# Order of the first loads and operations, of one bias transpose and of the last scatters in a graph-attention and mixture-of-experts kernel

## The chip, the cores and the metric

The kernel runs on one core of a Trainium2 chip. The metric is the time of one execution on the device, in microseconds, lower is better. The core has five engines that run side by side, each in the order of its own instruction list: PE (TensorE, matrix multiplication), DVE (VectorE), ACT (ScalarE), POOL (GpSimd) and SP (SyncE, which here only issues transfers). Engines wait for one another through semaphores. Transfers (DMA) are issued from the lists of SP, ACT and POOL, and they run beside all engines.

## The reference

There are N = 4096 rows of D = 256 numbers, an adjacency matrix of N x N integers, 4 attention heads of 64 columns, and 8 experts of 1024 hidden columns, of which each row uses 2.

```
xn   = layernorm(x)
h    = xn @ W                      per head
w_ij = exp(leaky_relu(s_row_i + s_col_j)) where adj_ij > 0, else 0
out  = (w @ h) / sum_j w_ij
y    = elu(out) + xn @ Wr + br
x    = x + layernorm(y) * gamma + beta
xf   = layernorm(x)
top two experts of xf @ Wg + bg, softmax over the two
x    = x + sum over the two of  share * (gelu(xf @ W1 + b1) @ W2 + b2)
```

## The kernel before, in words

**Attention.** The rows whose attention is computed are taken in four groups of 1024 (index `a`), each of two halves of 512. For a group the kernel walks over 32 tiles `j` of 128 neighbours. For each tile SP loads a slice of the transposed adjacency matrix (`load_adj`, 512 KB), ACT makes a mask of zeros and ones from it in two passes (`load_mask`, L1092 and L1093), DVE makes the weights `w` of four heads (`weigh`, L1205), and PE adds up `acc` (L745) and the denominators `den` (L754). The weights need `er`, the row scores of the group spread over all partitions. These are stored in memory as `parts` and loaded back over all partitions (`load_rows`, L710).

The projections `h`, the scores and the residual are computed in blocks of 512 rows (index `b`). Their work is woven into the first group: block b + 2 is normalised and turned (`norm_block`: moments by BNStats at L174, an inverse root in twelve short dependent DVE steps at L157 to L166 and L562, `xn`, PE transposes `pt` at L584, copies `xT` on ACT), and block b + 1 is projected (`project_block`: `ph`, `pr`, `ha`, `rb`).

**Start.** Blocks 0 and 1 have code of their own. DVE takes the moments of block 0 while its rows arrive; PE runs 37 matmuls without use (`WARM`) meanwhile. `scores_weights` folds the score vectors into the weights and computes `limit`, a bound on the scores, by one PE product (`plim`, L513), a root, and `flag`. `project_first` projects block 0 (L658), makes the scores, stores them (`store_parts`, L703), and scales `ha` (L676). `measured(1)` takes the moments and root of block 1, and `norm_block(1)` turns it. `residual_first` makes block 0's residual `rb` (PE `pr` at L688, DVE at L692). Then the program branches on `flag` (L1129) into general code, or into the code that runs here. In it, the first group's tiles j = 0 to 3 run for the first half of the rows alone, with masks kept in part of `er1`. After block 1 is projected and its scores are stored, the second `er` load brings the other half.

**Experts.** Each row goes into the lists of its two experts in memory. Tiles of 256 or 384 listed rows (jobs) run through both products (`up` with `ph` at L1355 and gelu at L1359; `down` with `po` at L1384), DVE scales the result and adds the bias (`o`, L1393), and POOL adds it to the output rows by an indirect transfer (scatter, L1396), 128 rows each, each after the one before has landed. The fixed number of jobs (`todo`) is followed by a branch for further jobs, which isn't taken here. The last scatter of the last fixed job stands behind this branch: `down` yields before it, and the generator is taken up again at the end of the program.

**What sets the order.** A scheduler at build time puts each engine's instructions in one fixed list, by the order in which the program issues them and by what they depend on. `tc.issue_after(x)` lets a group of operations count as issued after instruction `x` in that sorting; it adds no wait. On the first 40 us each engine's list is thus the result of the order of calls in the source and of these marks. PE's order in the attention is fixed by `queue`.

Of the kernel before, what the change touches and what calls it, by code (L numbers as in the profile page):

```python
# [1 line left out]

# [7 lines left out]
F32 = mybir.dt.float32  # L10
I32 = mybir.dt.int32
BF16 = mybir.dt.bfloat16
# [29 lines left out]
def gat_then_moe(  # L42
# [92 lines left out]
    def rows_of(mat, b):  # L135
        return mat[ts(b, B), :].rearrange("(t p) d -> p t d", p=P)
# [73 lines left out]
    def loaded(name):  # L210
        return fin.tile([P, TB, D], F32, tag="loaded", name=name, bufs=2)
# [253 lines left out]
    with ExitStack() as layer:  # L465
# [60 lines left out]
        first_masks = er1[:, 0].rearrange("p h r -> p (h r)").bitcast(BF16)  # L526
        first_masks = first_masks.rearrange("p (t r) -> p t r", t=TB)

        ha = gat.tile([P, NT, HK], F32)


# [14 lines left out]

        turned = {}

        def measured(b):

            xb = loaded("xb")
            if b == 0:
                for t in range(TB):
                    nc.sync.dma_start(xb[:, t, :], x[ts(t, P), :])
            else:
                nc.sync.dma_start(xb, rows_of(x, b))
            mv = moments(xb)
            r, _ = root_of(mv[:, :, 1], TB)
            off = None
            if b < 2:  # L560
                off = sums_of("off")
                marks["off"] = nc.vector.scalar_tensor_tensor(  # L562
                    off, mv[:, :, 0], -1.0, r, op0=OP.mult, op1=OP.mult
                ).ins
            return xb, mv, r, off

        def norm_block(b, found=None):

            xb, mv, r, off = found or measured(b)
            pt = [bank([P, B], f"pt{c}") for c in range(DC)]  # L570
            for t in range(TB):
                xn = fin.tile([P, D], F32, tag="xn", name="xn", bufs=2)
                if off is not None:
                    nc.scalar.activation(
                        xn, xb[:, t, :], AF.Identity, bias=off[:, t : t + 1],
                        scale=r[:, t : t + 1],
                    )
                else:
                    nc.vector.tensor_scalar(
                        xn, xb[:, t, :], mv[:, t, 0:1], r[:, t : t + 1],  # L580
                        op0=OP.subtract, op1=OP.mult,
                    )
                for c in range(DC):
                    nc.tensor.transpose(pt[c][:, ts(t, P)], xn[:, ts(c, P)], ident)  # L584
            xT = (first_large if b < 2 else large)("xT")
            xT = xT.rearrange("p t d -> p (t d)").rearrange("p (c i) -> p c i", c=DC)
            for c in range(DC):
                marks[f"turned{b}"] = nc.scalar.activation(  # L588
                    xT[:, c, :], pt[c], AF.Copy, accum_out=sums[:, c, b : b + 1]
                ).ins  # L590
            turned[b] = xT
# [59 lines left out]
        def project_first():  # L651

            sc = small.tile([P, TB, 2 * H], F32, tag="sc", name="sc")
            cols, rows = sc[:, :, :H], sc[:, :, H:]
            phs = [acc[t // 2][t % 2][:, : HK + 2 * H] for t in range(TB)]
            for t in range(TB):
                for c in range(DC):
                    nc.tensor.matmul(  # L658
                        phs[t], turned[0][:, c, ts(t, P)], wall[:, c, :],
                        start=(c == 0), stop=(c == DC - 1),  # L660
                    )
                nc.vector.tensor_tensor(rows[:, t], phs[t][:, HK + H :], limit, OP.add)
                nc.vector.tensor_tensor(
                    cols[:, t], phs[t][:, HK : HK + H], limit, OP.subtract
                )
            part = small.tile([P, H, TB], F32, tag="part", name="part")
            nc.vector.tensor_scalar(
                part.rearrange("p h t -> p t h"), rows, 0.0, None, op0=OP.max
            )
            nc.scalar.activation(part, part, AF.Exp, scale=SLOPE - 1.0)  # L670
            store_parts(0, part, nc.sync)
            ed = unit[:, :TB, :, 1]
            nc.scalar.activation(ed, cols, AF.Exp, scale=SLOPE)
            nc.scalar.activation(eb[:, :TB, :], cols, AF.Exp, scale=1.0 - SLOPE)
            for t in range(TB):
                marks["h"] = nc.vector.tensor_tensor(  # L676
                    ha[:, t, :].rearrange("p (h k) -> p h k", h=H),
                    phs[t][:, :HK].rearrange("p (h k) -> p h k", h=H),
                    ed[:, t].unsqueeze(2).to_broadcast([P, H, K]), OP.mult,
                ).ins  # L680
# [403 lines left out]
            last[0] = None  # L1084
            listed.clear()

        def load_mask(a, j, am=None):

            at = load_adj(gat, range(a * R, (a + 1) * R), j, 1, 3)
            if am is None:  # L1090
                am = gat.tile([P, R], BF16, tag="am", name="am", bufs=3)
            nc.scalar.activation(am, at[:, 0], AF.Relu)  # L1092
            nc.scalar.activation(am, am, AF.Sign)  # L1093
            return am


        idle = bank([P, B], "idle")
        for i in range(WARM):
            nc.tensor.matmul(
                idle, all1, all1[:, :1].to_broadcast([P, B]), start=(i == 0), stop=(i == WARM - 1)  # L1100
            )


        warm = gat.tile([P, 1], F32)
        nc.scalar.activation(warm, tiny, AF.Exp)
        marks = {}
        norm_block(0)
        with tc.issue_after(marks["off"]):
            scores_weights()
        project_first()  # L1110
        with tc.issue_after(marks["turned0"]):
            for j in range(2):
                load_mask(0, j, first_masks[:, j])
        with tc.issue_after(marks["flag"]):
            second = measured(1)

            nc.vector.tensor_scalar(brm, brm, -1.0, None, op0=OP.add)
            made_of_numbers()
        with tc.issue_after(marks["h"]):
            norm_block(1, second)  # L1120
            residual_first()
        load_rows(er0[:, :1], 0, 1, nc.sync)
        rest_of_loads()
        general = nc.values_load(
            flag[0:1, 0:1], min_val=0, max_val=1,
            skip_runtime_bounds_check_because="a comparison gives 0 or 1",
# [65 lines left out]
        with chosen.Else():  # L1192
# [4 lines left out]
            with tc.tile_pool(name="sep", bufs=2) as work:  # L1197
# [13 lines left out]
                    return w  # L1211

                both = list(range(HB))
                turn_biases()
                ers = [er0, er1]
                er = er0
                pending = None
                for a in range(NR):
                    later = None
                    for j in range(NT):  # L1220
                        if a == 0 and j % TB == 0 and j // TB + 2 < NB:
                            norm_block(j // TB + 2)
                        if a == 0 and j < TB:

                            am = first_masks[:, j]
                            if j > 1:
                                load_mask(a, j, am)
                            attend(weigh(er, am, j, [0]), j, [0])
                            if j == TB - 1:
                                project_block(1, True)  # L1230
                                load_rows(er[:, 1:], 1, 1, nc.sync)
                                for i in range(TB):
                                    attend(weigh(er, first_masks[:, i], i, [1]), i, [1])
                            continue
                        if a == 0 and j % TB == 0 and j // TB + 1 < NB:
                            project_block(j // TB + 1, True)
                        attend(weigh(er, load_mask(a, j), j, both), j, both)
                        if pending and j:
                            next(pending, None)
                            if j % 2 and a + 1 == NR:  # L1240
                                next(pending, None)
                        if a + 1 == NR and j == 29:
                            first_tile()
                        if j == 20 and a + 1 < NR:
                            later = ers[(a + 1) % 2]
                            load_rows(later, (a + 1) * HB, HB, nc.scalar)
# [116 lines left out]

    rounds, optional = [0], [False]

    def down(job, hT):


# [8 lines left out]
        for k in range(nch):  # L1377
# [8 lines left out]
                ))  # L1386
            if k + 1 == nch:
                yield
            if job["last"] and k + 1 == nch:
                o = work.tile([CH, D], F32, name="o_last", bufs=1)  # L1390
            else:
                o = work.tile([CH, D], F32, tag="o", name="o", bufs=2 * LAG - 2)
            given_out.append(nc.vector.scalar_tensor_tensor(  # L1393
                o, po, share[:, k : k + 1], b2s[k], op0=OP.mult, op1=OP.add
            ).ins)
            nc.gpsimd.indirect_dma_start(  # L1396
                job["into"], bass.IndirectOffsetOnAxis(ap=ids[:, k : k + 1], axis=0), o, None,
                compute_op=OP.add,
            )

    fresh()
    ordered[0] = True
# [102 lines left out]
```

## Time and profile before

| | us |
|---|---|
| time, median of 3 runs | 1325.94 |
| lowest, highest | 1325.19, 1327.08 |
| span of the profiled execution | 1330.1 |
| first scores weighted (`w`, L1205) | 34.81 |
| end of the attention, start of the experts | about 826 |
| last scatter starts | 1324.69 |

The profile is one execution, and its span is the frame of all times below. "Busy" is the share of the span in which an engine executes. In the slices each digit is a fortieth of the span (33 us), in tenths. In a chain of work each line is a start, a duration and what ran or was waited for; "issue" is time in which an engine waited for nothing that the profile shows. In a timeline a line is a start, a duration, the engine, the line of the program, what is written from what, and in brackets how long the engine had been idle and who ended that.

### The profile page before, as it was taken

The numbers are of one execution on the slowest core, as the hardware profiler recorded it, in microseconds if no ns is written. First come the engines' busy times: TensorE is split into PE (matmuls) and PEld (weight loads), VectorE is DVE, ScalarE is ACT, GpSimd is POOL, SyncE is SP. The second block draws the span as 40 slices with busy tenths as digits, with TensorE's granted clock in tenths as the row PEclk, the third lists the DMA queues.
The fourth block names the chain that finished last, engine by engine and source line by source line (L and its number), as shares of the span: only waits on it lengthen the run. The fifth ranks groups of instructions, "written<-read, shape, count | busy, mean of one in ns | idle before, by whom it ended". The sixth has DMA issues, their size and how long they took to land.

```text
span 1330.1 us, 19232 instructions
## 1 busy us (share of the span) xinstructions
PE 1287.9 (97%) x7019; PEld 679.3 (51%) x7019; DVE 868.8 (65%) x1746; ACT 574.1 (43%) x1016; POOL 232.5 (17%) x190
## 2 busy tenths in 40 slices
PE   6899999999999999999999999999999999999997
PEld 4423344322232222232222323888888877888886
DVE  4899887789999989999899996655111111121110
ACT  3423333346764457644576432533333332323332
POOL 1000000000005300015000150125222222122222
PEclk9899999999999999999999999999899999999999
DMA  5525243343443535534333342987756786888772
GB/s 164 204 84 174 96 111 96 112 158 100 131 136 109 194 98 140 138 107 153 96 111 111 106 133 60 350 249 213 245 155 188 189 183 146 197 203 209 175 208 53
DMA packets 144145, 202.42 MB, mean 152 GB/s; under 512 B 49728, under 2 KB 113872, under 8 KB 143392
## 3 DMA queue, kind: packets, MB, share of 16 engines
q1 hardware_dynamic: 122448, 161.26, 40.7%
q0 software_dynamic: 19360, 32.53, 10.9%
q10 hardware_dynamic: 2224, 7.22, 1.4%
q8 instruction: 59, 0.97, 0.3%
q14 instruction: 54, 0.44, 0.1%
HBM read 171.89 MB, written 29.08 MB: 151 GB/s over the span
## 4 chain that ended last, share of the span: by engine, by line
PE 57%; DMA 19%; DVE 17%; issue 5%; ACT 1%; another core or an unknown queue 0%; POOLq 0%; ACTq 0%; DVEq 0%
PE acc L745 24%; DMA out<-o,ids 18%; PE den L754 12%; DVE w L1205 12%; PE po L1384 8%; PE ph L1355 7%; PE pr L629 1%; PE ph L605 1%; DMA xb<-in_x 1%; DVE y L983 1%; DVE y L975 1%; PE pt L584 1%; DVE y L972 1%; PE pt L1337 1%; DVE y L989 0%
## 5 line engine op out<-in xcount | busy, mean ns | idle before, releaser
L1205 DVE SCALAR_TENSOR_TENSOR w<-er,eb,am 128x1024 f32<-128x1024 f32 x496 | 610.0, 1286 | 44.5 <-PE den L754 41.3
L745 PE MATMUL acc<-w,ha 128*64 128x512 f32 x2048 | 466.2, 599 | 5.3 <-DVE w L1205 4.6
L745 PEld LDWEIGHTS acc<-w,ha 128*64 128x64 f32 x2048 | 137.7, 137 | 301.6 <-issue 281.0
L1359 ACT ACTIVATE hT<-ph,bias 128x256 f32<-128x256 f32 (+1 forms) x264 | 126.3, 480 | 296.5 <-PE ph L1355 205.2
L1092 ACT ACTIVATE am<-adj 128x1024 bf16<-128x1024 int32 x124 | 131.1, 1057 | 283.8 <-DVE w L1205 275.2
L1355 PE MATMUL ph<-xT,w 128*128 128x256 f32 (+1 forms) x1056 | 242.3, 387 | 4.0 <-ACT hT L1359 2.5
L754 PE MATMUL den<-w,unit 128*2 128x512 f32 x2048 | 238.2, 592 | 5.5 <-DVE w L1205 5.5
L1384 PE MATMUL po<-w,hT 128*128 128x256 f32 x1088 | 241.9, 381 | 0.0
L1384 PEld LDWEIGHTS po<-w,hT 128*128 128x128 f32 x1088 | 206.7, 191 | 28.2
L1355 PEld LDWEIGHTS ph<-xT,w 128*128 128x128 f32 x1056 | 200.5, 190 | 39.4 <-ACT hT L1359 3.1
L1393 DVE SCALAR_TENSOR_TENSOR o<-po,share,b2s 128x256 f32<-128x256 f32 x67 | 32.3, 483 | 268.3 <-PE po L1384 246.8
L1396 POOL DMA_INDIRECT out<-o,ids x67 | 104.9, 1566 | 345.0 <-DMA out<-o,ids 215.6
L754 PEld LDWEIGHTS den<-w,unit 128*2 128x2 f32 x2048 | 43.5, 84 | 174.5 <-issue 151.8
L1093 ACT ACTIVATE am<-am 128x1024 bf16<-128x1024 bf16 x124 | 130.9, 1057 | 3.0
L909 POOL DMA_INDIRECT lists<-xe,at x64 | 92.0, 1437 | 134.3 <-DVE missed L888 39.5
L993 POOL DMA_DIRECT2D out<-y x6 | 4.7, 782 | 329.3 <-issue 155.6
L1341 DVE COPY xT<-pt 128x256 f32<-128x256 f32 x13 | 5.5, 423 | 66.3 <-PE pt L1337 66.3
L605 PE MATMUL ph<-wall,xT 128*128 128x264 f32 x112 | 30.6, 393 | 0.3 <-DVE sc L615 0.3
L1376 ACT ACTIVATE b2s<-b2b,share 128x256 f32<-128x256 f32 x68 | 30.8, 503 | 0.0
L629 PE MATMUL pr<-wr,xT 128*128 128x256 f32 x112 | 29.0, 384 | 0.2 <-ACT xT L588 0.2
L187 ACT ACTIVATE m<-y,off 128x256 f32<-128x256 f32 x48 | 23.8, 497 | 10.5 <-DVE off L184 10.5
L962 ACT ACTIVATE y<-ptr,z 128x64 f32<-128x64 f32 x96 | 22.0, 313 | 8.7 <-PE ptr L960 8.7
(316 smaller groups left out, 655.8 us busy)
## 6 DMA issues: line engine op xcount, KB each, us to landing
w<-in_L_ffn_W SPq DMA_DIRECT2D x66, 1024.0 KB
adj<-in_adj SPq DMA_DIRECT2D x128, 512.0 KB
er<-parts ACTq DMA_DIRECT2D x3, 2048.0 KB
b2b<-in_L_ffn_b SPq DMA_DIRECT2D x33, 128.0 KB
early<-lists SPq DMA_DIRECT2D x16, 260.0 KB
residual<-rb POOLq DMA_DIRECT2D x8, 512.0 KB
rb<-residual SPq DMA_DIRECT2D x8, 512.0 KB
out<-y POOLq DMA_DIRECT2D x8, 512.0 KB
```

Of the source, the lines that this page charges most:

```text
L605: nc.tensor.matmul(ph, xT[:, c, ts(t, P)], wall[:, c, :], start=(c == 0), stop=(c == DC - 1),)
L629: nc.tensor.matmul(pr[:, t % 2, :], xT[:, c, ts(t, P)], wr[:, c, :], start=(c == 0), stop=(c == DC - 1),)
L745: queue(nc.tensor.matmul(acc[half][h // 2][ts(h % 2, K), :], ha[:, j, ts(h, K)], w[half][h], start=(j == 0), stop=(j == NT - 1),))
L754: queue(nc.tensor.matmul(den[h * Q : h * Q + HB, :], unit[:, j, h, 1 - half : 1 - half + HB], w[half][h], start=(j == 0 and half == 0), st ...
L909: ins = nc.gpsimd.indirect_dma_start(lists, bass.IndirectOffsetOnAxis(ap=at[:, k, t : t + 1], axis=0), xe[:, t, :], None,).ins
L1092: nc.scalar.activation(am, at[:, 0], AF.Relu)
L1093: nc.scalar.activation(am, am, AF.Sign)
L1205: nc.vector.scalar_tensor_tensor(wh[:, these], er[:, these, h], eb[:, j, h : h + 1], mask[:, these], op0=OP.max, op1=OP.mult,)
L1355: order_of(nc.tensor.matmul(ph, job["w1"][:, c, ts(f, P)], xT[:, c, :], start=(c == 0), stop=(c == DC - 1),))
L1359: job["gelu"] = nc.scalar.activation(hT[:, f, :], ph, AF.Gelu, bias=job["bias"][:, f : f + 1]).ins
L1384: order_of(nc.tensor.matmul(po, hT[:, f, ts(k, CH)], w2[:, f, :], start=(f == 0), stop=(f == FC - 1)))
L1396: nc.gpsimd.indirect_dma_start(job["into"], bass.IndirectOffsetOnAxis(ap=ids[:, k : k + 1], axis=0), o, None, compute_op=OP.add,)
```

## The change

1. On SP, block 1's rows are loaded (`rows_loaded(1)`) ahead of the adjacency tiles j = 0 and 1. The tiles j = 2 and 3 of the first group, loaded after the branch before, are loaded at the start in one transfer of 1 MB, into a free half of `er1` (`first_adj`). `load_mask` is split so that the masks can be made from either place.
2. The matmuls without use become `warm_up`, which writes to `acc[1][1]` instead of a bank of its own; four more stand behind row tile 1's transposes of block 0 and two more behind row tile 3's. In PE's list `plim` is now behind all transposes of block 0.
3. `ha` of block 0 goes into `factor_first`, behind block 1's moments and root in DVE's list.
4. `residual_first` is called before `norm_block(1)`: in PE's list its eight `pr` products stand ahead of block 1's transposes.
5. `rest_of_loads` gets a mark; its place in POOL's list stays the same.
6. `turn_biases` (one PE transpose and one DVE copy) moves from just behind the branch into the second group, a = 1, at j = 1.
7. The last job's first scatter is held back until the branch for further jobs is passed, and goes out just ahead of the last one. It gets an output tile of its own, and the other `o` tiles have 9 buffers instead of 10.

```diff
+        first_adj = er1[:, 1].rearrange("p h r -> p (h r)").bitcast(I32)
+        first_adj = first_adj.rearrange("p (t r) -> p t r", t=2)
...
+        def warm_up(n):
+            idle = acc[1][1]
+            for i in range(n):
+                nc.tensor.matmul(
+                    idle, all1, all1[:, :1].to_broadcast([P, B]), start=(i == 0), stop=(i == n - 1)
+                )
...
+                if b == 0 and t % 2:
+                    with tc.issue_after(ins):
+                        warm_up(5 - t)
...
         norm_block(0)
+        second = rows_loaded(1)
         with tc.issue_after(marks["off"]):
             scores_weights()
         project_first()
+        with tc.issue_after(marks["off"]):
+            ats = [load_adj(gat, range(R), j, 1, 3) for j in range(2)]
+            nc.sync.dma_start(first_adj, adjT[2 * P : 4 * P, :R].rearrange("(t p) i -> p t i", p=P))
         with tc.issue_after(marks["turned0"]):
             for j in range(2):
-                load_mask(0, j, first_masks[:, j])
+                mask_of(ats[j][:, 0], first_masks[:, j])
         with tc.issue_after(marks["flag"]):
-            second = measured(1)
+            second = measured(1, second)
             nc.vector.tensor_scalar(brm, brm, -1.0, None, op0=OP.add)
             made_of_numbers()
+        with tc.issue_after(marks["off"]):
+            factor_first()
         with tc.issue_after(marks["h"]):
+            residual_first()
             norm_block(1, second)
-            residual_first()
         load_rows(er0[:, :1], 0, 1, nc.sync)
-        rest_of_loads()
+        with tc.issue_after(marks["turned0"]):
+            rest_of_loads()
...
-                turn_biases()
...
                             if j > 1:
-                                load_mask(a, j, am)
+                                mask_of(first_adj[:, j - 2], am)
...
+                        if a == 1 and j == 1:
+                            turn_biases()
...
             if k + 1 == nch:
                 yield
-            if job["last"] and k + 1 == nch:
-                o = work.tile([CH, D], F32, name="o_last", bufs=1)
+                while job["last"] and held_back:
+                    held_back.pop(0)()
+            if job["last"]:
+                o = work.tile([CH, D], F32, name=f"o_last{k}", bufs=1)
             else:
-                o = work.tile([CH, D], F32, tag="o", name="o", bufs=2 * LAG - 2)
+                o = work.tile([CH, D], F32, tag="o", name="o", bufs=2 * LAG - 3)
...
-            nc.gpsimd.indirect_dma_start(
-                job["into"], bass.IndirectOffsetOnAxis(ap=ids[:, k : k + 1], axis=0), o, None,
+            add = partial(
+                nc.gpsimd.indirect_dma_start, job["into"],
+                bass.IndirectOffsetOnAxis(ap=ids[:, k : k + 1], axis=0), o, None,
                 compute_op=OP.add,
             )
+            if job["last"] and k + 1 < nch:
+                held_back.append(add)
+            else:
+                add()
```

## The prediction

> **What bounds the kernel now.** I read the page first (busy shares, then the slices), next the chain of work in order of time for the first 40 us and for the end, and then the timeline of single engines there. The sums below are made against the profiled span, 1330.1 us; the three timed runs have a median of 1325.94 us (1325.19 to 1327.08), so I carry differences over and not totals. A timed change of 0.2%, 2.7 us, is about what these runs can tell from none.
>
> ```profile
> span 1330.1 us, 19232 instructions
> PE 1287.9 (97%) x7019; PEld 679.3 (51%) x7019; DVE 868.8 (65%) x1746; ACT 574.1 (43%) x1016; POOL 232.5 (17%) x190
> PE   6899999999999999999999999999999999999997
> DVE  4899887789999989999899996655111111121110
> ```
>
> PE is nearly always busy except in the first slice and the last; DVE is as full as PE through the attention (to about 826 us). Work that both start earlier therefore ends earlier: the place to look is the beginning. The chain there, then DVE's timeline:
>
> ```profile
> 23.49 0.69 PE pt L584 x2
> 24.17 0.85 PE pr L688 x2
> ...
> 28.21 2.01 PE pr L688 x8
> 30.22 0.02 issue
> 30.25 0.56 DVE rb L692
> 30.80 0.08 issue
> 30.88 0.07 DVEq L1129
> 30.95 3.75 issue
> ...
> 34.81 0.75 DVE w L1205
> ```
>
> ```profile
> 20.73 0.18 DVE L667 TENSOR_SCALAR part<-sc 128x16 f32<-128x16 f32 x1
> ...
> 22.64 0.16 DVE L562 SCALAR_TENSOR_TENSOR off<-mv,r 128x4 f32<-128x4 f32 x1
> 28.02 0.69 DVE L692 TENSOR_TENSOR rb<-pr,brm 128x512 f32<-128x512 f32 x1 [5.22 <-PE pr L688]
> 30.25 0.69 DVE L692 TENSOR_TENSOR rb<-pr,brm 128x512 f32<-128x512 f32 x1 [1.53 <-PE pr L688]
> 34.81 0.75 DVE L1205 SCALAR_TENSOR_TENSOR w<-er,eb,er 128x512 f32<-128x512 f32 x1 [3.87 <-issue]
> ```
>
> To be seen: DVE's last work before the branch (L1129) is the residual of block 0, `rb`. It waits 5.22 + 1.53 us for PE, whose `pr` matmuls stand between and behind block 1's transposes `pt`, and those wait for block 1's root (`off`, 22.64). Only after the branch and 3.75 us without an instruction can the first `w` start. The DMA rate falls to 8 GB/s between 27 and 28 us, so the 1 MB load of `er` (issued 23.21) has landed by then and is not what DVE waits for.
>
> The end, first the chain, then POOL's timeline:
>
> ```profile
> 1286.42 36.37 DMA out<-o,ids
> 1322.79 0.10 POOLq L1465
> ```
>
> ```profile
> 1308.53 1.54 POOL L1396 DMA_INDIRECT out<-o,ids  x1 [2.86 <-DMA out<-o,ids]
> 1317.93 1.55 POOL L1396 DMA_INDIRECT out<-o,ids  x1 [7.87 <-DVE o L1393]
> 1324.69 1.54 POOL L1396 DMA_INDIRECT out<-o_last,ids  x1 [5.21 <-issue]
> ```
>
> The scatter issued at 1317.93 lands at 1322.79; only then does POOL leave the branch, and the last scatter starts 1.90 us later, though its data `o_last` was written from 1320.79 on. From there to the end it is 1330.1 - 1324.69 = 5.4 us.
>
> **What the Trainium skill says.** "Runtime: NRT & Kernel Launch", section Instruction fetch mechanics: a taken branch to code outside the pages held forces a fetch before execution goes on. The trace agrees: 3.75 us on DVE here, and SP's branch at 24.1 is followed by its next load at 28.73. It gives no price, so I use 3.75. "TensorE: Matmul & The Clock Gate", What's actually happening: an idle PE drops to half clock and needs a busy window to return; the trace shows a granted clock of 0.54 from 36 to 41 us and 1.00 from 41 to 50. "DMA: Bandwidth & Descriptors", Rules for kernel authors: an accumulating DMA must wait for an earlier one on the same bytes; the trace agrees (42 scatters waited for the one before), so the last two stay serial.
>
> **The change, part by part.** Orders are those of the two built programs.
>
> *Loads.* On SP, block 1's `x` (512 KB) moves ahead of the two adjacency loads, and a 1 MB load for j = 2, 3 follows them. Before, it was issued at 6.86 and kept DVE waiting 1.72 us (to 16.92). The new order issues it at about 5.1, so it no longer binds. The extra 1 MB takes about 3 us at the 343 to 377 GB/s seen there and is in by about 18, under the projection and ahead of the `er` load. POOL's five small loads keep their place: 0.
>
> *Warm-ups.* Six more, at 10.75/37 = 0.29 us each. Four stand before the transposes of rows 2 and 3, which waited till 13.49 for their input and for `plim` anyway: 0 to +0.1. Two stand before `plim`, now last: it runs at about 14.75 and not 13.05, so DVE's root and `flag` end near 17.0 instead of 15.20, and BNStats of block 1 starts at 17.0 (before 16.92, for the DMA). The earlier load's gain is thus spent: 0.
>
> *Roots ahead of h.* From 17.0 DVE runs four BNStats (0.40 each), the score pairs (0.14) and `brm` (0.26) interleaved; PE's eight projections (3.96 us, from 15.1) end at 19.05. The last pair is at 19.4 and `part` at 19.6 (before 20.73: -1.1). Twelve dependent root steps at 0.20 end `off` at 21.9 (before 22.80: -0.9). Then four `ha` (1.42) to 23.4.
>
> *Residual ahead of block 1's transposes.* PE does `pp` at 20.0 and eight `pr`: 16 records at 0.22 to 0.25 = 3.5 to 4.0 us, from 20.3 to about 24.1. DVE's `rb` run 23.4 to 24.0 and 24.15 to 24.8. DVE branches at about 24.9 instead of 30.88: **-6.0**. Block 1's transposes follow on PE and ACT only; their second bank waits for the first `rb` (24.0), and ACT ends near 27.9 (before 28.74). SP stores `parts` 1.25 us earlier (20.6) and `er` lands at about 25.8, before it is needed; POOL's store of `rb` (512 KB, 31.24) moves ahead with its data to about 25.2 and has nothing behind it until block 1's. With the same 3.75 us of fetch the first `w` starts at 29.0 instead of 34.81: **-5.8**. The biases' copy leaves DVE here (0.14) and returns in the second attention block behind `z`, where DVE is the bound, with one 0.24 us matmul and a 0.22 us copy: net +0.1 to +0.4, taken as +0.2.
>
> *From there to the second half of the rows.* ACT's four mask passes (1.05 each) after its branch end near 36; the first is needed by the ninth `w`, at 36.1: just in time. SP's two `x` and six adjacency loads leave from 27.5 at 300 to 400 GB/s; none is needed before about 33. DVE's order up to the stored scores of block 1 holds 16 half `w` (0.65), two blocks' moments, eight normalisations and two roots, as before, but some eight root steps fewer ahead of it: before, 34.81 to 59.31 = 24.5 us; now about 23.5. `part` of block 1 comes at about 52.6 (before 59.31: -6.7). SP then issues block 5's `x`, when block 3's rows are normalised, and the second `er` load:
>
> ```profile
> 61.78 0.39 SPq L556 DMA_DIRECT2D xb<-in_x  x1
> 62.22 0.82 SPq L710 DMA_DIRECT2D er<-parts  x1
> ```
>
> These move to about 54.7 and 55.3. `x` lands 4.7 us later as before (66.44), and 2.7 us of DVE work lead to `w` on the new rows, which started at 69.04: now about 62. From this `w` on both programs issue the same instructions on DVE and PE, except for the biases, so the shift of **-7.0** stays to the end. PE's own limit caps the gain: in the stretches from 40 to 80 it was idle 1.34 + 0.77 + 1.36 = 3.5 us, so 5.8 + 3.5 = 9.3 is the most.
>
> *Tail.* The first of the last job's scatters moves behind the branch. POOL then leaves the branch when the scatter of 1308.53 has landed (about 4.9 us later, 1313.4) plus 1.9, at 1315.3, ahead of the data (1317.65). The first scatter starts at 1317.93 as before and lands at 1322.79; the next waits for that alone, and such pairs follow at 0.75 us (landing to start elsewhere in the chain): 1323.54 instead of 1324.69, **-1.1**. One `o` buffer fewer (9): comparing each `o` with the landing nine scatters earlier leaves at least 33 us; 0.
>
> Sum: -7.0 + 0.2 - 1.1 = -7.9, 1322.2 of the profiled span, or 1325.94 - 7.9 = **1318 us**.
>
> **The rivals.**
> A, the sum above: 0.65, own range 1316 to 1320.
> B, half the start comes back: `ha` and `rb` go out earlier, but masks j = 2, 3 or the fetch are late. The fetch was 4.6 us on SP under load against 3.75; ACT's masks have no slack. Each us late costs one; at 3 to 4 us, 1321.5. 0.18.
> C, the start was hidden: then only the tail counts, 1325 (same). For it: DVE and PE both fill the first block. Against: both start earlier. 0.09.
> D, slower: PE's clock. After the branch PE is fed by DVE and starts cold again after some 4 us of idling. If it stays at half clock, some 30 us of PE work up to 62 us become the bound. Each us at half clock loses 0.5 us; the gain of 7.9 and PE's 2 us of slack are gone after about 20 us more at half clock, and 30 us more make 1331. Against: before, the clock was back within 5 us. 0.05.
> That the held scatter delays the end is smaller: the first would have to start after 1319.1 to lose anything, and after 1327 to undo the start, against 1315.3 for POOL's exit. With other losses it makes 0.03, on the slower side too.
>
> **How the numbers follow.** A and B are faster: 0.83, and C's better half adds 0.03: 0.86. C's rest is the same, 0.06; D and the tail are slower, 0.08. Range: 1314.5 (PE's limit, 9.3 + 1.1, and the timed spread) to 1322.5 (B's worse end); outside it lie C, D and little else.
>
> **What would show it.** Right: DVE's `rb` of block 0 ahead of 25 us, first `w` at about 29, `w` on the second rows at about 62, later groups of equal duration; the last two scatters 5.6 us apart, the second starting 6 us before the end. Wrong: `rb` still waiting for PE after 27, BNStats of block 1 after 18, ACT's masks or PE's granted clock holding `w` between 30 and 60, or POOL's first held scatter more than 1 us after its `o`.

## The result

The changed kernel takes 1320.08 us (median of 4 runs, 1317.26 to 1321.65) against 1325.57 us for the kernel before (median of 4, 1324.7 to 1327.08). The ratio is 0.9955, with a 95% interval of 0.9935 to 0.9975. A second measurement beside three experiments gave 0.9941 (0.9922 to 0.9960). So it is faster by about half a per cent; 1318 was forecast.

The page of the changed kernel, its span, busy shares and the slices of PE and DVE:

```profile
span 1319.9 us, 19242 instructions
PE 1284.2 (97%) x7025; PEld 677.7 (51%) x7025; DVE 868.7 (66%) x1746; ACT 574.4 (44%) x1016; POOL 232.8 (18%) x190
PE   7999999999999999999999999999999999999996
DVE  6899877789999989999899997665111111121110
```

PE is as full as before in every slice but the first and the last. The two profiled spans are 10.2 us apart, more than the medians, and not all of that is the change's. About 5 to 6 us are one stall in the profiled execution of the kernel before, among the experts, here in its chain of work:

```profile
928.14 0.47 ACT hT L1359
928.61 3.12 another core or an unknown queue
931.73 0.03 issue
931.76 0.48 ACT hT L1359
```

ACT stood 3.12 us for something the trace does not name, and PE, idle meanwhile, came back at a lower clock (0.65 to 0.67 from 930 to 940 us). From the first `pt` of the experts to the end of PE's last `po` that execution needs 493.8 us; all others profiled for this study, experiment 8 apart, need 487.7 to 489.0. Later times of the kernel before are therefore compared as differences from a point of the same execution.

**The start.** DVE's timeline and the chain of work of the changed kernel:

```profile
18.88 0.18 DVE L688 TENSOR_SCALAR part<-sc 128x16 f32<-128x16 f32 x1
...
21.13 0.16 DVE L579 SCALAR_TENSOR_TENSOR off<-mv,r 128x4 f32<-128x4 f32 x1
...
22.54 0.68 DVE L717 TENSOR_TENSOR rb<-pr,brm 128x512 f32<-128x512 f32 x1
24.08 0.69 DVE L717 TENSOR_TENSOR rb<-pr,brm 128x512 f32<-128x512 f32 x1 [0.87 <-PE pr L713]
```

```profile
24.72 0.07 DVEq L1160
24.79 3.29 issue
28.08 0.05 DVEq L1236
28.13 0.06 issue
28.19 3.41 DVE w L1236 x5
31.60 0.09 issue
31.69 3.68 PE acc L770 x8
35.38 2.97 PE den L779 x16
```

DVE branches at 24.72 (30.88 before) and starts `w` at 28.19 (34.81 before), 6.6 us earlier. But the chain then hands over to PE, whose first `acc` starts at 31.69, only 4.7 us earlier than before (36.41), although it needs no more than the second `w`, which ended at about 29.5. (Before, it had started 0.1 us behind the second `w`.) PE's timelines, one line of the kernel before and two of the changed one, put the wait down to `w`:

```profile
36.41 3.68 PE L745 MATMUL acc<-w,ha 128*64 128x512 f32 x8 [3.10 <-DVE w L1205]
...
25.12 0.93 PE L601 MATMUL pt<-ident,xn 128*128 128x128 f32 x4 [0.64 <-ACT xn L591]
31.69 3.68 PE L770 MATMUL acc<-w,ha 128*64 128x512 f32 x8 [5.64 <-DVE w L1236]
```

What really held it is in the records of the branch on the engines' sequencers (duration as minimum, median and maximum in ns, then the start in us); the first line is of the kernel before, the rest of the changed one:

```profile
L1129 PEldq COMPARE_BRANCH  x1: 3931/3931/3931, 28.9 to 28.9; - x1
...
L1160 SPq COMPARE_BRANCH  x1: 45/45/45, 23.2 to 23.2; - x1
L1160 DVEq COMPARE_BRANCH  x1: 72/72/72, 24.7 to 24.7; - x1
L1160 POOLq COMPARE_BRANCH  x1: 50/50/50, 25.6 to 25.6; - x1
L1160 PEldq COMPARE_BRANCH  x1: 5317/5317/5317, 26.2 to 26.2; - x1
```

PE's branch begins at 26.2 and takes 5.32 us (28.9 and 3.93 before): PE is ready for its next instruction at 31.5. Just ahead of it POOL had issued the store of block 0's residual, 512 KB (POOL's timeline):

```profile
25.07 0.79 POOL L720 DMA_DIRECT2D residual<-rb  x1 [19.16 <-DVE rb L717]
```

**The end.** POOL's timeline:

```profile
1303.04 1.54 POOL L1440 DMA_INDIRECT out<-o,ids  x1 [2.98 <-DMA out<-o,ids]
1309.23 1.55 POOL L1424 DMA_INDIRECT out<-o_last,ids  x1 [4.65 <-issue]
1314.42 1.54 POOL L1440 DMA_INDIRECT out<-o_last,ids  x1 [3.64 <-issue]
```

The last two scatters are 5.19 us apart instead of 6.76. But the one before them starts 7.05 us after the start of its `o` (1295.99), where it was 1.71 us before the change, so POOL leaves the branch late and the first held scatter starts 2.4 us after its data are complete (1306.37 + 0.48). From the end of PE's last `po` (1309.71) it is 10.2 us to the end of the span, against 9.6 before.

### The profile page after: what moved, and what is told of

The parts are those of the page before. It is cut to its first block, busy times and chain, and to the rows that moved or that the text cites. A ratio compares the mean times of both kernels' runs of the same rounds, so it can differ in the third digit from the quotient of the medians.

```text
span 1319.9 us, 19242 instructions
## 1 busy us (share of the span) xinstructions
PE 1284.2 (97%) x7025; PEld 677.7 (51%) x7025; DVE 868.7 (66%) x1746; ACT 574.4 (44%) x1016; POOL 232.8 (18%) x190
## 4 chain that ended last, share of the span: by engine, by line
PE 60%; DMA 17%; DVE 16%; issue 4%; ACT 1%; POOLq 0%; ACTq 0%; DVEq 0%; SPq 0%
PE acc L770 24%; DMA out<-o,ids 15%; PE den L779 12%; DVE w L1236 12%; PE ph L1387 9%; PE po L1418 9%; PE pr L650 1%; PE ph L626 1%; DMA adj<-in_adj 1%; DVE y L1008 1%; DVE y L1000 1%; DMA er<-parts 1%; DVE y L997 1%; PE pt L1369 1%; DVE y L1014 0%
## 5 line engine op out<-in xcount | busy, mean ns | idle before, releaser
L1410 ACT ACTIVATE b2s<-b2b,share 128x256 f32<-128x256 f32 x68 | 30.8, 503 | 0.0
L626 PE MATMUL ph<-wall,xT 128*128 128x264 f32 x112 | 30.3, 392 | 0.5 <-DVE sc L636 0.3
```

Of the source, the lines that this page charges most:

```text
L626: nc.tensor.matmul(ph, xT[:, c, ts(t, P)], wall[:, c, :], start=(c == 0), stop=(c == DC - 1),)
```

## The experiments

The landmarks read from each trace: "ready" is when PE's branch is over, "second w" the end of the second `w` (the start of the first and 0.67 us for each, and for the biases' copy between them where it stands there). All in us.

| kernel | PE's branch: start, length | ready | second w | first acc | w, second rows | PE's end to span's end |
|---|---|---|---|---|---|---|
| before | 28.9, 3.93 | 32.8 | 36.3 | 36.41 | 69.04 | 9.6 |
| changed | 26.2, 5.32 | 31.5 | 29.5 | 31.69 | 64.31 | 10.2 |
| changed, again | 25.5, 5.31 | 30.8 | 28.8 | 30.95 | 63.11 | 8.0 |
| scatter back | 25.1, 5.23 | 30.3 | 28.3 | 30.48 | 62.31 | 9.8 |
| transposes first | 26.5, 3.82 | 30.3 | 34.4 | 34.62 | 67.17 | 10.2 |
| DVE late | 25.5, 5.20 | 30.7 | 31.5 | 31.70 | 64.21 | 8.1 |
| PE late | 26.5, 4.81 | 31.3 | 31.0 | 31.52 | 64.14 | 8.1 |
| store later | 25.6, 3.35 | 29.0 | 28.5 | 29.13 | 62.68 | 7.8 |
| store later, again | 26.4, 3.61 | 30.0 | 29.3 | 30.12 | 62.94 | 8.0 |
| residual first alone | 27.5, 4.85 | 32.3 | 33.8 | 33.92 | 67.13 | 9.7 |
| tail alone | 27.4, 3.85 | 31.2 | 35.5 | 35.60 | 68.26 | 14.8 |

In all eleven the first `acc` starts 0.1 to 0.3 us after the later of the two, PE's readiness and the second `w`. One start differs from one execution to the next. Scatter back and experiment 8 leave the start of the changed kernel as it is, so four profiles have it: their first `acc` lies between 30.18 (experiment 8) and 31.69, their second rows between 62.31 and 64.31. Differences of one trace below 1 to 2 us are therefore not read.

**1. Scatter back: the tail undone in the changed kernel**

```diff
-            if job["last"] and k + 1 < nch:
-                held_back.append(add)
-            else:
-                add()
+            add()
```

> The changed kernel with the last job's first scatter issued ahead of the branch again, as before the change; its nine buffers stay. Theory (the tail is worth what the prediction said): the two last scatters are 6.6 us apart or more instead of 5.2, the span ends 1.0 to 1.1 us later, and nothing moves ahead of 1300 us. Rival (the scatters have a queue of their own that is late anyway, so that holding one back gives nothing): the last scatter starts within 0.3 us of the same time after PE's last matmul.

Measured: ratio to the kernel before 0.9961 (0.9948 to 0.9973). POOL's timeline:

```profile
1305.11 1.55 POOL L1437 DMA_INDIRECT out<-o_last,ids  x1 [6.34 <-DVE o_last L1429]
1311.95 1.54 POOL L1437 DMA_INDIRECT out<-o_last,ids  x1 [5.29 <-issue]
```

They are 6.84 us apart again, and from PE's end it is 9.8 us. With the held scatter, and where POOL had caught up (DVE late, PE late, both "store later", the changed kernel again), it is 7.8 to 8.1. Without it, before the change and with the residual first alone, it is 9.6 and 9.7. So the tail is worth 1.5 to 2.0 us, more than expected, in executions where the scatters are at most some 3 us behind their data. The time alone can't tell it.

**2. Transposes first: step 4 undone**

```diff
-            residual_first()
             norm_block(1, second)
+            residual_first()
```

> The changed kernel with block 1's normalisation and transposes ahead of the residual of block 0 again; all else as changed. Theory F (PE's own instruction fetch behind the branch sets the start of the first acc, 31.69 in the changed kernel, and with it all that follows): PE's branch at about 28.0 instead of 26.2, its fetch again 4 to 5 us, the first acc at 33 to 35, the first w on the second half of the rows 2.5 to 3.5 us later than 64.31. Theory V (the vector engine's first w sets it): rb at about 29.3, first w at about 33.5 instead of 28.19, and the second rows 5.3 us later.

Measured: ratio 0.9970 (0.9959 to 0.9981); `rb` at 25.70 and 27.93, first `w` at 33.06, second rows 2.9 us later than in the first profile of the changed kernel, 2.9 to 4.9 us later than in the four with its start. Here PE was ready at 30.3 and waited for DVE. The second rows came as F expected; but PE branched at 26.5 and not at 28, and the first `acc` was DVE's doing. Both of my theories were too simple, for which of the two comes last depends on the order. It also showed a PE branch of 3.82 us where the store of `rb` is behind it.

**3. DVE late, 4. PE late**

```diff
             residual_first()
+            spare = gat.tile([P, 32], F32)
+            nc.vector.tensor_copy(spare, brm[:, :32])
+            for i in range(6):
+                nc.vector.tensor_scalar(spare, spare, 1.0, None, op0=OP.mult)
             norm_block(1, second)
```

> The changed kernel with seven small dependent operations (0.2 us each) on DVE between the residual of block 0 and the branch, so that DVE branches some 1.4 us later; nothing else waits for them. Theory F (PE's fetch sets the start): first w 1.4 us later, at about 29.6, but the first acc within 0.4 us of 31.69 and the first w on the second rows within 0.4 us of 64.31. Theory V (DVE's first w sets it): both 1.4 us later.

Measured: ratio 0.9959 (0.9945 to 0.9973). First `w` at 30.15, 2.0 us later than in the changed kernel, and yet the first `acc` at 31.70 and the second rows at 64.21. These are the numbers of F, but in part by chance: in this execution PE was ready at 30.7, and the second `w` (31.5) came last. So 2 us are a little more than DVE has to spare, and the run agrees with "the later of the two" rather than with F alone.

```diff
             norm_block(1, second)
+            warm_up(4)
```

> The changed kernel with four more idle matmuls (0.29 us each) on PE among block 1's transposes, ahead of PE's branch only. Theory F: PE's branch, its first acc and the first w on the second rows come 0.5 to 1.2 us later (part of it lies in PE's wait for xn). Theory V: first acc and second rows within 0.3 us of 31.69 and 64.31, since DVE's first w does not move.

Measured: ratio 0.9949 (0.9937 to 0.9961). PE's branch came 4.4 us after the first `rb` (3.7 in the changed kernel), but was over in 4.81 us, and DVE's first `w` came late too (29.66). PE ready at 31.3, the second `w` at 31.0: this run does not tell the theories apart.

**5. Store later, twice**

```diff
             rb = residuals("rb")
...
-            nc.gpsimd.dma_start(rows_of(residual, 0), rb)
+            return rb
...
-            residual_first()
+            kept = residual_first()
             norm_block(1, second)
+            store = nc.gpsimd.dma_start(rows_of(residual, 0), kept)
+            after(store.ins, marks["turned1"], "the store goes behind block 1")
```

> The changed kernel with POOL's 512 KB store of block 0's residual held until ACT has copied block 1's transposes (about 27.1 instead of 25.07), so that it no longer goes out just ahead of PE's instruction fetch. Theory S (the store stands in front of PE's fetch; runs with it in front show 4.8 to 5.3 us of fetch, those without it 3.8 to 3.9): PE's fetch 3.8 to 4.2 us, the first acc 0.15 us after it and 1.0 to 1.4 us earlier than 31.69, the first w on the second rows 32.6 us after that first acc; the whole 1 to 1.4 us shorter than the changed kernel, unless block 2's x, now behind the store, takes some of it. Rival (five engines fetch at nearly the same time and the load of er is in front): PE's fetch 5 us or more as before, no gain.

> The changed kernel with the store of block 0's residual held behind block 1's copies, a second time, on the same chip as the changed kernel. Theory S: PE's fetch again under 4 us, against 4.8 to 5.3 in the changed kernel; the first w on the second rows 36.8 to 37.3 us after PE's branch, against 37.6 to 38.1; some 1 us (0.08%) less than the changed kernel. Rival (the short fetch was chance): a fetch of 4.8 us or more here too.

Measured: ratios 0.9945 (0.9927 to 0.9962) and, on the chip where the changed kernel has 0.9941 (0.9922 to 0.9960), 0.9944 (0.9924 to 0.9963). The branch records of the first and the second run:

```profile
L1162 PEldq COMPARE_BRANCH  x1: 3351/3351/3351, 25.6 to 25.6; - x1
```

```profile
L1162 PEldq COMPARE_BRANCH  x1: 3607/3607/3607, 26.4 to 26.4; - x1
```

3.35 and 3.61 us, against 4.75 to 5.32 in all eight profiles in which that store goes out ahead of PE's branch (experiments 7 and 8 are among them, with 4.89 and 4.75), and 3.82 to 3.93 in the three in which it comes after. One thing moved with the store and is a rival: POOL's own branch, which follows the store in POOL's list. It comes 0.5 to 1.1 us ahead of PE's in the eight profiles and behind PE's in the other five. Experiment 6 below speaks against it, for there POOL branches 7 us ahead of PE and PE's branch is long all the same. The DMA packets of the traces speak for the store. In every profile one packet of 16 KB on an instruction queue starts within PE's branch and ends 1.2 to 1.7 us before PE is ready, so I take it for PE's fetch. Without the store ahead it starts 0.94 to 1.32 us after the branch begins. With the store ahead it starts after 1.99 to 2.51 us, at 28.49 in the changed kernel, where the store's packets run from 26.45 to 28.53; in six of the eight profiles it starts in the last 0.1 us of the store's packets, in DVE late and PE late 0.5 and 1.1 us before their end. So PE's fetch stood behind the store: the edit and the packets agree.

It is worth less than it looks. The first `acc` starts 3.5 and 3.8 us after PE's branch begins, against 5.5 in the two runs of the changed kernel, but the second rows 37.1 and 36.6 us after it, against 38.1 and 37.6. In scatter back and experiment 8, which have the changed kernel's start, it is 37.2 and 37.3. On the means 0.7 us is left, and none that the time can tell. One of DVE's waits, first in the changed kernel, then in the first of the two runs, between 26 us and the second rows (total, times, longest):

```profile
DVE st L175 <- DMA xb<-in_x: 2.1, 3, 1.0
...
DVE st L175 <- DMA xb<-in_x: 2.5, 3, 1.3
```

DVE waits about as long for the blocks' `x` as in the changed kernel (2.1 us in the second profile of that kernel, 1.9 in the second of these runs). The load of block 2's `x` can only leave when SP has fetched its own instructions behind the branch: it branched at 22.6 and issued that load at 26.92. What else took up the rest is not settled.

**6. Residual inside: all of `residual_first` behind the branch**

```diff
-            residual_first()
             norm_block(1, second)
...
                 both = list(range(HB))
+                residual_first()
```

> The changed kernel with the whole residual of block 0 (eight pr, two rb, the store) behind the branch: PE and DVE branch some 2 us earlier, and PE does the pr while it would wait for w. Theory S: with no store ahead of it PE's fetch takes 3.8 to 4.2 us. Theory on PE's clock (PE comes out of the fetch at half clock, so the pr take twice 3.5 us): first acc at about 34 to 35, but at full clock from there, so that the second rows come within 1.5 us of 64.31 and the time is the changed kernel's within 1.5 us. Rival (the branch is all that counts): first acc at 29 to 30 and 2 us gained.

Measured: ratio 0.9944 (0.9923 to 0.9964). PE branched at 23.6, but took 5.27 us, with no store ahead; so S as I stated it fails here. The 1 MB load of `er`, issued at 21.86, was under way instead: its large packets run from 22.82 to 26.43, and PE's 16 KB packet starts at 26.36, 2.75 us after the branch. So it is the same wait behind another transfer, as far as packets show it; no run took that load away. PE's timeline:

```profile
29.05 5.60 PE L713 MATMUL pr<-wr,xT 128*128 128x256 f32 x16 [5.34 <-SPq L1543]
34.58 1.94 PE L770 MATMUL acc<-w,ha 128*64 128x512 f32 x8
```

The 16 `pr` records take 5.60 us where they took 3.62 before the branch: they pay for the half clock (granted 0.50 from 24 to 32 us in this run, 1.00 from 34), and the eight `acc` behind them take 1.94 us instead of 3.68. Second rows at 64.16, as the clock theory expected. Here the cold start is paid once, by what comes first. "TensorE: Matmul & The Clock Gate", What's actually happening, says that PE needs a busy window to return to full clock; in the changed kernel the granted clock was 0.50 from 28 to 36 us and 1.00 from 38.

**7. No warm-ups: the six extra idle matmuls left out**

```diff
-                if b == 0 and t % 2:
-                    with tc.issue_after(ins):
-                        warm_up(5 - t)
```

> The changed kernel without the six idle matmuls among block 0's transposes. If they cost what the prediction said: plim and flag come 0.6 to 1.3 us earlier, but BNStats of block 1 then waits for its x or starts up to 0.8 us earlier; branches and first acc move by less than 0.7 us, and the time by less than 0.7 us. If they keep PE's clock up for the projections: PE's granted clock falls to half between 13 and 20 us, the eight projections take up to 7 us instead of 3.83, and everything behind them comes 1 to 3 us later.

Measured: ratio 0.9948 (0.9928 to 0.9968); `flag` at 14.87 instead of 16.34, PE's clock 1.00 from 8 to 22 us, branches of DVE and PE within 0.4 us of the changed kernel's. They neither cost nor bring anything that can be seen.

**8. Zeros on SP**

```diff
-                ends[0:1, e : e + 1], engines=[mybir.EngineType.Pool],
+                ends[0:1, e : e + 1], engines=[mybir.EngineType.SP],
...
-            nc.gpsimd.dma_start(
+            nc.sync.dma_start(
                 lists[bass.ds(end, WT), :].rearrange("(p c) d -> p (c d)", p=CH), zeros
```

> The changed kernel with the eight stores of zeros at the lists' ends issued by SP instead of POOL, where they hold up the scatters for about 9 us (929.38 to 938.72). Theory Q (the scatters are a serial queue of their own that starts about 25 us late and catches up only near the end; what is left at the end is paid): the scatter that waited behind the zeros starts some 9 us earlier, the lag of the scatter before the last job's falls from up to 7.0 us to 0.8 to 2, and from PE's last matmul to the end it is 8.1 us instead of 10.2; at most 2 us faster, and PE's time from the end of the attention to its last matmul stays 487.7 us. Rival: SP then waits for the lists itself, a weight load comes late and PE waits for it in the experts, so that it is slower by some us.

Measured: slower than before, ratio 1.0030 (1.0019 to 1.0040). The scatters did catch up: the first behind the zeros starts at 922.5 instead of 939.6, and it is 7.4 us from PE's end to the span's. But SP, which issues the experts' loads, stood: it issued none between 905.8 and 921.4 us, and PE soon stood with it:

```profile
921.81 8.43 PE L1387 MATMUL ph<-xT,w 128*128 128x256 f32 x30 [3.37 <-DVE xT L1373]
...
938.83 7.14 PE L1387 MATMUL ph<-xT,w 128*128 128x256 f32 x32 [1.24 <-DMA w<-in_L_ffn_W]
```

From the attention's end to PE's last `po` it takes 495.7 us. The rival was right.

**9. Residual first alone, in the kernel before**

```diff
+            residual_first()
             norm_block(1, second)
-            residual_first()
```

> The kernel before with one edit of the change alone, the residual of block 0 ahead of block 1's normalisation and transposes; loads, roots, biases and scatters stay. Undoing this edit in the changed kernel cost 3.0 us at the first acc, so if the edits add up: first acc 3 to 4 us earlier than 36.41 and the second rows as much earlier than 69.04, 3 to 3.8 us in all. PE's fetch then has the store in front: 4.8 to 5.3 us. Rival (it needs the earlier roots and loads): DVE's rb is early, but masks j = 2, 3, which are still loaded behind the branch, hold w, and less than 2 us is left at the second rows.

Measured: ratio 0.9981 (0.9967 to 0.9995), the second rows 1.9 us earlier than in the profile before, 1.1 us earlier than in the tail-alone run. DVE's timeline behind the branch:

```profile
29.45 0.75 DVE L1205 SCALAR_TENSOR_TENSOR w<-er,eb,er 128x512 f32<-128x512 f32 x1 [3.32 <-ACT xT L588]
32.98 0.23 DVE L232 COPY bT<-pb 128x64 f32<-128x64 f32 x1 [2.78 <-PE pb L231]
```

The edits do not add up: DVE is early, but its second instruction behind the branch copies the turned biases, which PE makes only when it has fetched (ready at 32.3). So `w` waits 2.78 us. The rival's size came, though masks were not what held it. Moving `turn_biases` away is part of what makes the new order pay.

**10. Tail alone, in the kernel before, and the changed kernel again**

```diff
+                while job["last"] and held_back:
+                    held_back.pop(0)()
...
+            if job["last"] and k + 1 < nch:
+                held_back.append(add)
+            else:
+                add()
```

> The kernel before with the held scatter and the nine buffers of the change alone. Theory (prediction's tail): all as before up to PE's last matmul, except for chance; the last two scatters 5.2 to 5.6 us apart instead of 6.8, and from PE's last matmul to the end 8.1 us instead of 9.6, if the scatters have caught up by then: 1.1 to 1.6 us less. Where the last but two scatter is over 2 us behind its data, the first held one starts late and 10 us or so are left: nothing gained. Rival: no difference in either case.

> The changed kernel once more, unaltered, beside the next three: PE's fetch 4.8 to 5.3 us, from the first acc to the first w on the second rows 31.8 to 32.7 us, from there to the end of the attention 757.7 us, from there to PE's last matmul 487.7 us, and from that to the end 8.1 us where the scatters have caught up, up to 10.2 us where they have not. Ratio to the kernel before 0.9945 to 0.9960.

Measured: tail alone 1.0004 (0.9984 to 1.0025). Its chain of work near the end:

```profile
1294.53 23.08 DMA out<-o,ids
1317.61 0.10 POOLq L1475
...
1318.80 3.68 DMA out<-o_last,ids
```

Scatters, each behind the one before, carry the chain from 1294.53 on. PE had ended at 1314.65, and its end to the span's end is 14.8 us: the scatter before the last job's started 11.7 us after its `o`, so the first held one had to wait. In the changed kernel run again that lag was 2.5 us and the rest 8.0 us. Its first `acc` and second rows came 0.7 and 1.2 us earlier than in the first profile, and its PE took 488.9 us for the experts.

## Why the prediction was right or wrong

**Loads and warm-ups, 0: right.** BNStats of block 1 started at 16.41 (17.0 foretold), and without the warm-ups the time is the same.

**Roots ahead of `ha`, -1.1 at `part`, -0.9 at `off`: right, a little small.** They moved by 1.85 and 1.5 us.

**Residual ahead of the transposes, -6.0 at DVE's branch and -5.8 at its first `w`: right.** The branch is at 24.72 (24.9 foretold), `w` at 28.19 (29.0).

**That the stage starts with DVE's first `w`: the step that failed.** I let the first `w` at 29.0 stand for the start of the whole stage. The first `acc` moved by 4.7 us. I gave DVE the fetch of 3.75 us that its trace showed, and did not ask when PE comes back, whose 3.93 us stood in the trace before with 3.1 us of waiting behind it. With DVE 6.6 us earlier and PE's branch only 2.7, PE was last, and it is last in all four profiles with this start (ready at 30.0 to 31.5, the second `w` at 28.3 to 29.5). And of the store of `rb` I wrote that it "has nothing behind it": PE's instruction fetch was behind it, and grew by 1.4 us.

**-6.7 at `part`, by some eight root steps fewer on DVE: did not come.** `part` came at 54.04, 5.3 us earlier: 22.4 us after the first `acc`, against 22.9 before. The chain of work runs through PE's `acc` and `den` from 31.69 to 44.77, at half clock up to about 37, and through a load of `x` from 45.94 to 50.29: these set the pace, not DVE's count.

**-7.0 at the second rows: measured -4.7 in these two profiles.** What stands behind `part` moved with it: block 5's `x` left 5.0 us earlier (56.74), and DVE's work on it ended 4.9 us earlier, at 64.10. The second `er` load added the last 0.2 us (kernel before, then changed):

```profile
69.04 3.40 DVE L1205 SCALAR_TENSOR_TENSOR w<-er,eb,er 128x512 f32<-128x512 f32 x5
...
64.31 3.40 DVE L1236 SCALAR_TENSOR_TENSOR w<-er,eb,er 128x512 f32<-128x512 f32 x5 [0.21 <-DMA er<-parts]
```

The size hangs on the execution. The tail-alone kernel has the start of the kernel before. On the means of the profiles with each start (two and four) DVE's first `w` is 7.0 us earlier, the first `acc` 5.2 and the second rows 5.6 (68.65 and 63.07).

**The shift stays to the end: right for the attention.** From the first `w` on the second rows to the experts' first `pt` it is 757.7 us in both.

**Biases, +0.2: wrong in size and in sign.** In the second group they cost nothing visible (the 757.7 us just named), and where they were, experiment 9 shows them holding `w`, once DVE comes before PE.

**Tail, -1.1: the mechanism is right, the size hangs on POOL.** It is -1.5 to -2.0 where the scatters have caught up, and in the two profiles +0.6, since the changed one had a lag of 7 us. I had the sign for it ("first held scatter more than 1 us after its `o`"; it was 2.4), but took the lag of one execution, 1.71 us, for a property of the kernel.

**The sum.** From the two profiles, -4.7 and, from 9.6 to 8.0, -1.6 make -6.3; with the means of the start it is -7.2. Forecast were -7.9. So the start was 1.4 to 2.3 us too large, the tail 0.5 too small, and the 0.2 of the biases did not come. That the forecast time is as close as it is owes something to luck: these errors have opposite signs, and the tail can go either way from one execution to the next. Of the rivals, B is closest in mechanism (a late fetch gives back a part), but on PE, which it did not name; ACT's masks were done at 33.93 and held nothing. C and D did not come (no start was hidden, and the kernel is not slower), though D's cause, PE at half clock up to about 37 us, is part of what kept the first block's work from being shorter. The measured intervals, -0.65% to -0.25% and -0.78% to -0.40%, hold all three sums.

## What to carry to other kernels

When a branch must be fetched by every engine, list for each engine when it branches, how long its fetch takes and what it needs first; the stage starts with the last of these, and an engine made earlier only helps up to the next. A transfer that nobody waits for can still delay an engine, if it goes out just ahead of that engine's instruction fetch; here PE's fetch was 1.7 us longer for it (5.31 against 3.61 us on the same chip), of which some 0.7 us was left 37 us on. And before a lag at a serial queue's end is used as a number, look at more than one execution of it.

## What the runs showed of the hardware

PE's fetch behind the branch took 3.35 to 3.93 us when no large transfer was under way ahead of it and 4.75 to 5.32 us with a 512 KB store ahead of it; experiment 6 had 5.27 us with a 1 MB load. "Runtime: NRT & Kernel Launch", Instruction fetch mechanics, has it that such a fetch is made by DMA. The packets agree: PE's 16 KB packet starts about 1 us after the branch when the way is free, and about 2 to 2.8 us after it, near the end of the other transfer's packets, when it is not. Of the two transfers only the store was taken away.

The `er` load may do the same to SP and DVE in the changed kernel. They branch at 23.2 and 24.7, and the next two packets on the other instruction queue start at 26.22 and 26.24, in the last 0.4 us of `er`'s packets (to 26.62). Which engine a packet of that queue is for the trace does not say, so this stays open.

The serial scatters ran from 1.7 to 11.7 us behind their data at the last scatter but two, and in one and the same kernel, the changed one, 7.05 and 2.5 us. What makes one execution catch up and another not is not settled; one try at removing it, experiment 8, moved the wait to SP.
